# Two-operand VectorE steps of a routed two-layer network: `places` reckoned in a PSUM bank, `less` with an operand in PSUM, the sums of attention reduced

## The chip, the cores and the metric

The kernel runs on one core of one Trainium2 chip. The metric is the device time of one execution in microseconds (us). Names of engines in the profile: PE is TensorE's matmul, PEld its weight load, DVE is VectorE, ACT is ScalarE, POOL is GpSimd, SP is SyncE, which only issues DMAs here. SBUF is the large on-chip memory and PSUM the small one that TensorE writes to, in eight banks of 512 floats per partition.

## The reference, cut to what matters

`x` is (4, 384, 32, 32): four batches of 384 channels at 1024 places ("tokens"). There are two layers, each with a mixing part and a feed-forward part, all in float32:

```
x = x + scan(ln_channels(x))               # selective scan, 4 directions, 16 states, then a norm and gelu
t = tokens(x)
t = t + experts(ln_tokens(t))              # 4 experts, each token goes to its best 2
x = image(t)
x = x + attention(ln_channels(x))          # 8 heads of 64, queries = keys = values
t = tokens(x); t = t + kron_mlp(ln_tokens(t))
```

The routing, which the change touches most, is in the reference:

```
probs = softmax(scores)                    # over the 4 experts
topk_vals, topk_idx = top_k(probs, 2)
mask = sum(one_hot(topk_idx, 4))
masked = probs * mask
masked = masked / (sum(masked) + 1e-9)
out = einsum('bse,ebsd->bsd', masked, y)   # y: what each expert makes of the token
```

Attention is `softmax(w w^T / 8) w` for each head.

## The kernel before, in words

**Two streams.** `scan_layer` goes through 32 units (4 batches, 4 directions, 2 halves of 512 tokens). For each unit, `project` makes the step sizes, and `chunk` runs over three channel groups of 128 and four groups of four states. One step of `chunk` is: POOL multiplies `bx <- dtr, bcs` (L432), ACT makes `da` by an exponential into PSUM (L441), DVE scans along the tokens (L446), DVE (L453) or POOL (L460) multiplies by the output coefficients, and PE adds the states up in `acc` (L467). When a batch is through the scan, `finish` writes it to `x1`, and `tail_batch` of the batch before is handed in: `route` (transposes, norm, `places`, then scattered writes to `rows`), `experts` (11 slots of 256 or 128 tokens), `combine`, `prologue` (norm), `attention`, and `last_layers`. So the tail of batches 0 to 2 runs beside the scan of later batches, and the tail of batch 3, with what is left of batch 2's, runs alone at the end. `route` of batch b + 1 is handed in between `attention` and `last_layers` of batch b.

**Order.** The order of each engine's instructions is fixed before the run by a planner, which goes by the order of the program text, priorities (route, combine, prologue and last_layers have a raised one) and its own reckoning of durations. Each engine works its queue in order. A buffer or a bank of a pool is handed on when the planner has put its last reader behind it.

**Banks.** While the scan runs, it holds four of the eight PSUM banks. The tail has the other four: one double bank "s", one bank "o" and one bank "p" (`NARROW_BANKS`). Bank "o" is used by `y_ps` of the experts, `o_acc` of attention and `f_acc` of `last_layers` (L1165, copied out at L1170). Bank "p" is used by many short-lived tiles, among them `tt_ps` and `cnt_ps` of the route and every second `h_ps` of the experts. For batch 3, `route` takes its tiles and banks from a second set that opens when the scan's banks are free.

**What the change touches.**
- `less_mean` (L540 to L544) makes `-mean * rstd`, a 128x8 tile, in one DVE instruction, L543. It is called eight times: in `spread` of each route (L649, where ACT's L659 uses it) and in `prologue` of each batch (where ACT's L960 uses it, and the transposes L967 wait for that).
- `places` (L676 on) takes the scores `sc` (128 partitions x 8 blocks of tokens x 4 experts) and works out, in some 60 small DVE instructions, the softmax, each expert's rank for each token (L698 to L703 compare all pairs of experts), the two chosen ones, how many tokens before this one go to each expert (two matmuls, L718 and L719, and a running sum, L725), how many slots each expert fills (L729 to L743), and from that the row of every token in `rows` (`pos`, L788), its weight, and each slot's expert (L794 to L814). All of its tiles are in SBUF but the result of the two matmuls. L647 and L648, just ahead of it, finish the scores.
- `divide` in `attention` adds two sums of each token and head with one DVE instruction (L1028) and takes the reciprocal (L1029); four calls a batch.

Of the kernel before, what the change touches and what calls it, by code (L numbers as in the profile page):

```python
# [12 lines left out]
ALU = mybir.AluOpType  # L13
AX = mybir.AxisListType
# [3 lines left out]
P = 128  # L18
# [13 lines left out]
NE = 4  # L32
TOP = 2
# [15 lines left out]
MB = L // P  # L49
# [61 lines left out]
def halves(i):  # L111
    return slice(i * HF, (i + 1) * HF)


class Body:
# [424 lines left out]
    def less_mean(self, mean, rstd, room, tag):  # L540

        less = room.tile([P, MB], tag, "less")
        self.nc.vector.scalar_tensor_tensor(less, mean, -1.0, rstd, op0=ALU.mult, op1=ALU.mult)  # L543
        return less  # L544


# [129 lines left out]
    def places(self, sc, room):  # L676


        nc = self.nc
        nt = MB  # L680

        def over(v):
            return v.unsqueeze(2).to_broadcast([P, nt, NE])

        red = room.tile([P, nt], "g_red", "g_red")
        nc.vector.tensor_reduce(red, sc, AX.X, ALU.max)
        nc.vector.tensor_sub(sc, sc, over(red))
        nc.scalar.activation(sc, sc, AF.Exp)
        nc.vector.tensor_reduce(red, sc, AX.X, ALU.add)
        nc.vector.reciprocal(red, red)  # L690
        nc.vector.tensor_mul(sc, sc, over(red))

        shape = [P, nt, NE, NE]
        mine = sc.unsqueeze(3).to_broadcast(shape)
        other = sc.unsqueeze(2).to_broadcast(shape)
        above = room.tile(shape, "g_above", "g_above")
        same = room.tile(shape, "g_same", "g_same")
        nc.vector.tensor_tensor(above, other, mine, op=ALU.is_gt)  # L698
        nc.vector.tensor_tensor(same, other, mine, op=ALU.is_equal)
        nc.vector.tensor_mul(same, same, self.lower.unsqueeze(1).to_broadcast(shape))  # L700
        nc.vector.tensor_add(above, above, same)
        rank = room.tile([P, nt, NE], "g_rank", "g_rank")
        nc.vector.tensor_reduce(rank, above, AX.X, ALU.add)  # L703
        chosen = room.tile([P, TOP, nt, NE], "g_chosen", "g_chosen")
        for k in range(TOP):
            nc.vector.tensor_scalar(chosen[:, k], rank, float(k), None, op0=ALU.is_equal)
        nc.vector.tensor_scalar(rank, rank, float(TOP), None, op0=ALU.is_lt)
        nc.vector.tensor_mul(sc, sc, rank)
        nc.vector.tensor_reduce(red, sc, AX.X, ALU.add)
        nc.vector.tensor_scalar_add(red, red, 1e-9)  # L710
        nc.vector.reciprocal(red, red)
        nc.vector.tensor_mul(sc, sc, over(red))


        ps = room.bank("p", "cnt_ps")
# [1 line left out]
        flat = rank.rearrange("p m e -> p (m e)")  # L717
        nc.tensor.matmul(ps[:, :n], self.before, flat, start=True, stop=True)  # L718
        nc.tensor.matmul(ps[:, n : 2 * n], self.ones, flat, start=True, stop=True)  # L719
        cnt = room.tile([P, 2, nt, NE], "g_cnt", "g_cnt")  # L720
        nc.vector.tensor_copy(cnt.rearrange("p t m e -> p (t m e)"), ps[:, : 2 * n])
        run = room.tile([P, nt + 1, NE], "g_run", "g_run")
        nc.vector.memset(run[:, 0, :], 0.0)
        for m in range(nt):
            nc.vector.tensor_add(run[:, m + 1, :], run[:, m, :], cnt[:, 1, m, :])  # L725

        ns = nt * P // P
        need = room.tile([P, NE, ns], "g_need", "g_need")
        nc.vector.tensor_tensor(  # L729
            need, run[:, nt, :].unsqueeze(2).to_broadcast([P, NE, ns]),  # L730
            self.full[:, :ns].unsqueeze(1).to_broadcast([P, NE, ns]), op=ALU.is_gt,
        )

        used = room.tile([P, 2, NE], "g_used", "g_used")
        nc.vector.tensor_reduce(used[:, 1], need, AX.X, ALU.add)
        nc.vector.tensor_reduce(used[:, 0], need[:, :, 1::2], AX.X, ALU.add)
        nc.vector.scalar_tensor_tensor(
            used[:, 1], used[:, 0], -2.0, used[:, 1], op0=ALU.mult, op1=ALU.add
        )
        first = room.tile([P, 2, NE + 1], "g_first", "g_first")  # L740
        nc.vector.memset(first[:, :, :1], 0.0)
        for e in range(NE):
# [5 lines left out]

        at = cnt[:, 0]
        nc.vector.tensor_add(at, at, run[:, :nt, :])  # L750
        shift = room.tile([P, 2, NE], "g_shift", "g_shift")
        full, back = shift[:, 0], shift[:, 1]
        nc.vector.tensor_scalar(
            back, odd[:, :NE], float(NHALF) - 0.5, -float((NHALF + 2) * P), op0=ALU.is_gt, op1=ALU.mult
        )
# [5 lines left out]
            op0=ALU.mult, op1=ALU.add,  # L761
# [6 lines left out]
        ends = room.tile([P, nt, NE], "g_ends", "g_ends")  # L768
# [5 lines left out]
            at, pairs[:, :NE].unsqueeze(1).to_broadcast([P, nt, NE]), float(SLOT), at,  # L774
            op0=ALU.mult, op1=ALU.add,
        )
        nc.vector.tensor_add(at, at, ends)
        pick = room.tile([P, 2, TOP, nt, NE], "g_pick", "g_pick")
        both = [P, TOP, nt, NE]
        nc.vector.tensor_mul(pick[:, 0], chosen, at.unsqueeze(1).to_broadcast(both))  # L780
        nc.vector.tensor_mul(pick[:, 1], chosen, sc.unsqueeze(1).to_broadcast(both))
        picked = room.tile([P, 2, TOP, nt], "g_picked", "g_picked")
        nc.vector.tensor_reduce(
            picked.rearrange("p t k m -> p (t k m)"),
            pick.rearrange("p t k m e -> p (t k m) e"), AX.X, ALU.add,
# [1 line left out]
        pos = room.sb.tile([P, TOP, nt], I32, tag="g_pos", name="g_pos", bufs=2)  # L787
# [24 lines left out]
        )  # L812
        expert = room.sb.tile([P, NSLOT], I32, tag="g_expert", name="g_expert", bufs=2)
        nc.vector.tensor_copy(expert, ef)  # L814
        return pos, picked[:, 1], expert

    def experts(self, b, routed, room):

# [155 lines left out]
    def attention(self, xc, sums, room):  # L974
# [5 lines left out]
        nc, a = self.nc, self.a  # L980
# [44 lines left out]

        def divide(t, att):
            inv = room.tile([P, 2 * MB], "inv", "inv")
            nc.vector.tensor_add(inv, sums[:, t, :, 0], sums[:, t, :, 1])  # L1028
            nc.vector.reciprocal(inv, inv)  # L1029
            ps = room.bank("p", "inv_ps")  # L1030
            nc.tensor.matmul(ps[: 2 * MB, :P], inv, self.ident, start=True, stop=True)
            rows = room.tile([2 * MB, P], "inv_rows", "inv_rows")
            nc.vector.tensor_copy(rows, ps[: 2 * MB, :P])
            for i in range(NH):
                ps = room.bank("p", "bc_ps")
                for j in range(HF // P):
                    m = i * (HF // P) + j
                    for o in range(2):
                        at = 2 * m + o
                        nc.tensor.matmul(  # L1040
                            ps[o * HD : (o + 1) * HD, j * P : (j + 1) * P],
                            self.ident[: 2 * MB, at : at + 1].to_broadcast([2 * MB, HD]),
                            rows, start=True, stop=True,
                        )
                nc.vector.tensor_mul(att[:, halves(i)], att[:, halves(i)], ps)
# [370 lines left out]
```

## Time and profile before

| | |
|---|---|
| three runs | median 4451.01 us, 4446.85 to 4462.27 |
| the profiled execution | 4452.07 us, its span from first to last instruction 4450.2 |
| mean granted clock of TensorE | 0.850 |
| PE busy | 3462.1 us, 78% of the span |
| POOL busy | 3050.0 us, 69% |
| DVE busy | 2980.1 us, 67% |
| ACT busy | 2469.7 us, 55% |

| stretch of the trace | from, to (us) |
|---|---|
| last scan instruction of batch 3 (L446) | ends at 3564.6 |
| experts of batches 0, 1, 2, 3 (L889) | start at 935.1, 1995.2, 3046.3, 3696.4 |
| attention's scores of batches 0, 1, 2, 3 (L1015) | 1462 to 1767, 2520 to 2816, 3567 to 3931, 4195 to 4352 |
| `places` (L687 to L788) | 848 to 895, 1872 to 1918, 2927 to 2972, 3645 to 3661 |
| L543 in the prologues | starts at 1426.0, 2485.5, 3536.3, 4176.5 |

A line of the profile such as "L453 DVE TENSOR_TENSOR bx<-da,bcs" names the line of the kernel, the engine, the operation, the tile that is written and the tiles that are read. Busy time does not tell of waiting inside an instruction: an instruction that has begun and can't go on counts as busy, and only its length gives it away.

### The profile page before, as it was taken

To read this page: it belongs to the slowest core of one execution; us is meant where nothing else is said; L and a number is where in the kernel's file an instruction comes from. 1 tells how busy PE (TensorE), PEld (TensorE's weight loads), DVE (VectorE), ACT (ScalarE), POOL (GpSimd) and SP (SyncE) were. 2 spreads that over 40 slices of the span, in tenths; PEclk is the share of its full clock that TensorE was granted. 3 is DMA by queue.
4 is the path that set the end of the run, shared out by engine and by line. 5 is a ranking of instruction groups with operands and counts; after the bars stand their busy time and mean duration, and the time that the engine had idled before them with its cause. 6 is when DMAs were issued, how large, how long until landed. Compare 5 with 4: busy or idle time off the path is not lost. (4 is left out here: it accounts for less than half of the span.)

```text
span 4450.2 us, 47090 instructions
## 1 busy us (share of the span) xinstructions
PE 3462.1 (78%) x13980; PEld 1644.5 (37%) x13980; DVE 2980.1 (67%) x4252; ACT 2469.7 (55%) x4380; POOL 3050.0 (69%) x1475
## 2 busy tenths in 40 slices
PE   6545554579995887669998688758998699999897
PEld 2111111245552222325555222214555334566333
DVE  5889998778887876978787777988787720020002
ACT  4545554456664766466666477466666453325354
POOL 4999999689988877779888689879888710000100
PEclk7766665579997998679999899869999899999898
DMA  4444453468785533357779434446778534344300
GB/s 121 119 124 114 129 162 91 134 225 233 217 253 169 164 93 116 117 174 217 209 229 274 134 99 120 123 145 193 215 212 261 171 106 139 123 135 164 102 17 15
DMA packets 404760, 684.81 MB, mean 154 GB/s; under 512 B 50960, under 2 KB 206480, under 8 KB 404496
## 3 DMA queue, kind: packets, MB, share of 16 engines
q1 hardware_dynamic: 395184, 655.37, 50.0%
q0 software_dynamic: 8192, 25.17, 1.7%
q8 instruction: 112, 1.84, 0.2%
q14 instruction: 152, 1.25, 0.1%
q10 hardware_dynamic: 1120, 1.18, 0.1%
HBM read 561.47 MB, written 120.06 MB: 153 GB/s over the span
## 5 line engine op out<-in xcount | busy, mean ns | idle before, releaser
L432 POOL TENSOR_TENSOR bx<-dtr,bcs 128x1024 f32<-128x1024 f32 x768 | 1793.5, 2362 | 211.5 <-PE acc L467 118.2
L441 ACT ACTIVATE da<-dtr,nega 128x512 f32<-128x512 f32 x1536 | 1045.8, 691 | 1013.9 <-DVE bx L453 637.7
L460 POOL TENSOR_TENSOR bx<-bx,bcs 128x1024 f32<-128x1024 f32 x384 | 904.0, 2360 | 216.9 <-DVE bx L446 94.9
L467 PE MATMUL acc<-bx,sel 128*32 128x512 f32 x3072 | 518.6, 712 | 304.2 <-POOL bx L460 258.4
L889 PE MATMUL h_ps<-xc,w 128*128 128x256 f32 (+1 forms) x3168 | 665.2, 364 | 43.6 <-DVE xc L871 21.1
L905 PE MATMUL y_ps<-w,hs 128*128 128x384 f32 x1824 | 644.1, 505 | 44.3 <-ACT hs L898 40.3
L889 PEld LDWEIGHTS h_ps<-xc,w 128*128 128x128 f32 x3168 | 547.4, 196 | 228.6 <-issue 92.0
L446 DVE TENSOR_TENSOR_SCAN bx<-da,carry,bx 128x512 f32<-128x512 f32 x384 | 473.9, 1269 | 125.1 <-ACT da L441 61.9
L446 DVE TENSOR_TENSOR_SCAN da<-da,carry,bx 128x512 f32<-128x512 f32 x384 | 477.3, 1273 | 70.6 <-ACT da L441 61.3
L446 DVE TENSOR_TENSOR_SCAN bx<-da,bx 128x512 f32<-128x512 f32 x384 | 451.8, 1209 | 102.6 <-POOL bx L432 61.3
L453 DVE TENSOR_TENSOR bx<-da,bcs 128x512 f32<-128x512 f32 x768 | 511.3, 680 | 4.5
L446 DVE TENSOR_TENSOR_SCAN da<-da,bx 128x512 f32<-128x512 f32 x384 | 455.7, 1219 | 74.5 <-ACT da L441 62.9
L905 PEld LDWEIGHTS y_ps<-w,hs 128*128 128x128 f32 x1824 | 348.6, 196 | 339.6 <-issue 78.2
L1020 ACT ACTIVATE ex<-s_ps 128x512 f32<-128x512 f32 x512 | 299.2, 590 | 207.1 <-PE s_ps L1015 206.1
L1015 PE MATMUL s_ps<-w 64*128 64x512 f32 x1024 | 307.6, 675 | 83.0 <-ACT ex L1020 83.0
L467 PEld LDWEIGHTS acc<-bx,sel 128*32 128x32 f32 x3072 | 78.6, 116 | 606.1 <-POOL bx L460 371.0
L1064 PE MATMUL o_acc<-ex,vt 128*64 128x512 f32 x1024 | 295.3, 657 | 0.6 <-ACT att L1072 0.5
L894 ACT ACTIVATE hs<-h_ps,bb 128x256 f32<-128x256 f32 (+1 forms) x528 | 193.6, 449 | 148.5 <-PE h_ps L889 148.3
L1105 POOL TENSOR_TENSOR xt<-xt,wb 128x3072 f32<-128x3072 f32 x4 | 26.7, 6686 | 310.4 <-DMA wb<-in_wb 310.4
L909 DVE TENSOR_TENSOR y<-y_ps,bb 128x384 f32<-128x384 f32 x76 | 41.6, 548 | 244.0 <-PE y_ps L905 244.0
L926 POOL TENSOR_TENSOR diag<-ident,g_picked 128x1024 f32<-128x1024 f32 x8 | 15.0, 1895 | 243.1 <-PE xc_ps L868 223.8
L1015 PEld LDWEIGHTS s_ps<-w 64*128 64x128 f32 x1024 | 80.9, 192 | 257.6 <-ACT ex L1020 153.4
(215 smaller groups left out, 4026.3 us busy)
## 6 DMA issues: line engine op xcount, KB each, us to landing
w<-in_w SPq DMA_DIRECT2D x352, 576.0 KB
dtr<-dd SPq DMA_DIRECT2D x1536, 128.0 KB
bcs<-rows SPq DMA_DIRECT2D x512, 128.0 KB
dd<-one_e SPq DMA_DIRECT2D x96, 256.0 KB
dd<-mag SPq DMA_DIRECT2D x96, 256.0 KB
rows<-zero SPq DMA_DIRECT2D x76, 192.0 KB
xs<-rows SPq DMA_DIRECT2D x32, 384.0 KB
made<-y SPq DMA_DIRECT2D x32, 384.0 KB
```

The costliest lines, as they stand in the source:

```text
L432: pool = nc.gpsimd.tensor_mul(bx, dtr[q][1], bc[:, 0].unsqueeze(1).to_broadcast([P, 2, HF])).ins
L441: nc.scalar.activation(da, dtr[q][0][:, j, :], AF.Exp, scale=nega[:, col : col + 1])
L446: nc.vector.tensor_tensor_scan(run(h), run(da), run(bx[:, j, :]), 0.0 if first else hold, ALU.mult, ALU.add,)
L453: dve = nc.vector.tensor_mul(bx[:, j, :], h, cg).ins
L460: pool = nc.gpsimd.tensor_mul(bx, bx, cg.unsqueeze(1).to_broadcast([P, 2, HF])).ins
L467: nc.tensor.matmul(acc[lo : lo + DB, :], sel, out[q][:, j, :], start=(g == 0), stop=(g == NG - 1),)
L889: nc.tensor.matmul(ps[:, r, :], w1[(f + r) // wf][:, c, (f + r) % wf * P : ((f + r) % wf + 1) * P], xc[:, c, :], start=(c == 0), stop=(c = ...
L894: nc.scalar.activation(hs[:, f + r, :], ps[:, r, :], AF.Identity, bias=bb[:, f + r : f + r + 1])
L905: nc.tensor.matmul(out[:, :D], hs[:, f, t * P : (t + 1) * P], w2[f // wf][:, f % wf, :], start=(f == 0), stop=(f == FC - 1),)
L1015: nc.tensor.matmul(ps[:, o, :], w[rows, j * P : (j + 1) * P], w[rows, halves(i)], start=True, stop=True,)
L1020: ins = nc.scalar.activation(ex[:, o, :], ps[:, o, :], AF.Exp, scale=HD**-0.5, accum_out=sums[:, t, 2 * j + o, i : i + 1],).ins
L1064: ins = nc.tensor.matmul(out[cols, :], made[t][1][:, j, cols], ex[:, o, :], start=(j == 0), stop=(j == MB - 1),).ins
```

## The change

The change keeps what is computed. It alters where some small tiles lie and which instructions make them.

- `less_mean`: ScalarE first copies `rstd` into a tile of bank "p", and L543 reads it from there.
- `places`: a tile of bank "o" (`area`) is taken at the start, and `small` hands out pieces of it one behind the other. `red`, a second copy of the probabilities (`prob`, by one more multiplication), `same`, `number` (the rank before it becomes the mask), `chosen`, `cnt`, `total` (the last step of the running sum, which was the last row of `run`), `used`, `back` and `picked` lie there. What pairs with them stays or moves into SBUF: `sc`, `above`, `rank`, `part`, `run`, `need`, `blocks`, `first`, `full`, `row`, `ends`, `pick`. The weights that are returned are copied out to SBUF (`weight`), one more instruction.
- `divide`: the addition of two slices of `sums` becomes a reduction over its last axis, which has two elements.

```diff
     def less_mean(self, mean, rstd, room, tag):
         less = room.tile([P, MB], tag, "less")
-        self.nc.vector.scalar_tensor_tensor(less, mean, -1.0, rstd, op0=ALU.mult, op1=ALU.mult)
+        ps = room.bank("p", "less_ps")[:, :MB]
+        self.nc.scalar.copy(ps, rstd)
+        self.nc.vector.scalar_tensor_tensor(less, mean, -1.0, ps, op0=ALU.mult, op1=ALU.mult)
...
+        area = room.bank("o", "places")
+        used_up = [0]
+
+        def small(shape):
+            lo = used_up[0]
+            used_up[0] = lo + int(np.prod(shape[1:]))
...
-        red = room.tile([P, nt], "g_red", "g_red")
+        red, prob = small([P, nt]), small([P, nt, NE])
...
+        nc.vector.tensor_mul(prob, sc, over(red))
         nc.vector.tensor_mul(sc, sc, over(red))
...
-        other = sc.unsqueeze(2).to_broadcast(shape)
+        other = prob.unsqueeze(2).to_broadcast(shape)
         above = room.tile(shape, "g_above", "g_above")
-        same = room.tile(shape, "g_same", "g_same")
+        same = small(shape)
...
-        nc.vector.tensor_reduce(rank, above, AX.X, ALU.add)
-        chosen = room.tile([P, TOP, nt, NE], "g_chosen", "g_chosen")
+        number = small([P, nt, NE])
+        nc.vector.tensor_reduce(number, above, AX.X, ALU.add)
+        chosen = small([P, TOP, nt, NE])
...
-        cnt = room.tile([P, 2, nt, NE], "g_cnt", "g_cnt")
+        cnt = small([P, 2, nt, NE])
...
-        for m in range(nt):
+        for m in range(nt - 1):
             nc.vector.tensor_add(run[:, m + 1, :], run[:, m, :], cnt[:, 1, m, :])
+        total = small([P, NE])
+        nc.vector.tensor_add(total, run[:, nt - 1, :], cnt[:, 1, nt - 1, :])
...
-        used = room.tile([P, 2, NE], "g_used", "g_used")
-        nc.vector.tensor_reduce(used[:, 1], need, AX.X, ALU.add)
+        used = small([P, 2, NE])
+        blocks = room.tile([P, NE], "g_blocks", "g_blocks")
+        nc.vector.tensor_reduce(blocks, need, AX.X, ALU.add)
...
-        shift = room.tile([P, 2, NE], "g_shift", "g_shift")
-        full, back = shift[:, 0], shift[:, 1]
+        full, back = room.tile([P, NE], "g_full", "g_full"), small([P, NE])
...
-        nc.vector.tensor_add(at, at, ends)
+        row = room.tile([P, nt, NE], "g_row", "g_row")
+        nc.vector.tensor_add(row, at, ends)
...
-        picked = room.tile([P, 2, TOP, nt], "g_picked", "g_picked")
+        picked = small([P, 2, TOP, nt])
...
-        return pos, picked[:, 1], expert
+        weight = room.tile([P, TOP, nt], "g_weight", "g_weight")
+        nc.vector.tensor_copy(weight, picked[:, 1])
+        return pos, weight, expert
...
         def divide(t, att):
             inv = room.tile([P, 2 * MB], "inv", "inv")
-            nc.vector.tensor_add(inv, sums[:, t, :, 0], sums[:, t, :, 1])
+            nc.vector.tensor_reduce(inv, sums[:, t], AX.X, ALU.add)
```

## The prediction

> **What bounds the kernel now.** I read the page's slices first, then the waits, then VectorE's (DVE's) rows one line at a time, and last the timeline of DVE and GpSimd (POOL) side by side.
>
> ```profile
> PE   6545554579995887669998688758998699999897
> ...
> DVE  5889998778887876978787777988787720020002
> ...
> POOL 4999999689988877779888689879888710000100
> ...
> ACT da L441 <- DVE bx L453: 637.7, 366, 9.8
> ```
>
> The first three are tenths of busy time in 40 slices of 111 us. Up to slice 32 (about 3600 us) the scan runs, DVE and POOL mostly at 7 to 9 tenths, neither full for long; after that TensorE is full and DVE and POOL stand nearly still. The last row, the longest wait, says who paces the scan: ScalarE idles 637.7 us until DVE frees a `da` buffer. So a microsecond that DVE loses before 3600 us is mostly lost to the end, and one after it hardly counts.
>
> DVE does lose some. The rows are min/median/max of one instruction in ns:
>
> ```profile
> L453 DVE TENSOR_TENSOR bx<-da,bcs x768: 649/679/696, 57.3 to 3564.6; 128x512 f32<-128x512 f32 x192
> ...
> L543 DVE SCALAR_TENSOR_TENSOR less<-mv,rstd x8: 152/164/12677, 847.6 to 4176.5; 128x8 f32<-128x8 f32 x8
> ...
> L1028 DVE TENSOR_TENSOR inv<-sums x16: 174/176/10531, 1535.6 to 4353.1; 128x16 f32<-128x16 f32 x16
> ...
> L743 DVE TENSOR_TENSOR g_first<-g_first,g_used x16: 145/163/2278, 879.8 to 3658.3; 128x2 f32<-128x2 f32 x16
> ```
>
> L453 reads `da` in PSUM and `bcs` in SBUF, 768 times beside a busy POOL, and never leaves 649 to 696 ns. The others have both operands in SBUF, and on eight, sixteen or two elements one takes up to 12.7 us. The timeline round the longest (start, length, then idle time before in brackets), DVE above, POOL below:
>
> ```profile
> 1426.00 12.68 DVE L543 SCALAR_TENSOR_TENSOR less<-mv,rstd 128x8 f32<-128x8 f32 x1 [0.61 <-ACT rstd L151]
> 1438.60 2.44 DVE L446 TENSOR_TENSOR_SCAN bx<-da,carry,bx 128x512 f32<-128x512 f32 x2
> ...
> 1425.90 4.63 POOL L432 TENSOR_TENSOR bx<-dtr,bcs 128x1024 f32<-128x1024 f32 x2
> 1430.51 1.25 POOL L388 TENSOR_TENSOR lnw<-lnw,mag 128x512 f32<-128x512 f32 x1
> 1431.73 6.92 POOL L432 TENSOR_TENSOR bx<-dtr,bcs 128x1024 f32<-128x1024 f32 x3
> 1441.19 2.35 POOL L460 TENSOR_TENSOR bx<-bx,bcs 128x1024 f32<-128x1024 f32 x1 [2.54 <-DVE bx L446]
> 1452.02 2.37 POOL L460 TENSOR_TENSOR bx<-bx,bcs 128x1024 f32<-128x1024 f32 x1 [8.48 <-DVE bx L446]
> ```
>
> DVE's 8-element instruction stands while POOL runs six in a row and ends as that run ends; then POOL starves for 2.54 and 8.48 us, waiting for the scans that DVE could not start. [...]
>
> **The change, part by part.** A stall below is a row's length less the shortest of its kind, from DVE's timeline. Only rows before 3600 us stall.
>
> *`less` (L543).* The four of the routes take 0.15 us; three of the prologues take 12.68, 11.62 and 10.80, stalls of 12.5, 11.5 and 10.6. With `rstd` in PSUM they have one SBUF operand, as L453. POOL worked meanwhile, so I count only what it idles afterwards: 11.0 (2.54 + 8.48), 8.8 (3.35 + 5.44) and 12.2, capped at 10.6: **30.4 us**. ScalarE's L960 of the layer behind the scan ("the tail") waits for `less` too (12.79 us idle), so both streams gain.
>
> *`inv` (L1028).* A reduce reads one operand. Its stalls are 1.7, 1.2, 2.2, 0.3 and 10.4 us; POOL idles 8.50 behind the last; of the other 5.4 I take half, the ends being 0 and 5.4: **11.2 us**. The reduce costs as the add (nearest row: L689's reduce, 166 ns, against 176).
>
> *`places`.* Each call has some 37 DVE instructions with two SBUF operands; five stay so (the two of L794, L806, L809, L810), and L647 ahead of it. Stalls that go: 15.0 us in the first call (L687, L698, L708, L743, L763 and others), 12.6 in the second, 15.3 in the third, none in the fourth, where POOL is idle. The three stretches, and one of the experts:
>
> ```profile
> core 0: us, PE busy (x) PEld busy (x) DVE busy (x) ACT busy (x) POOL busy (x), PEclk, DMA share, GB/s
> 843.00:897.00 54.00, 16.84 (x38) 3.54 (x38) 53.43 (x110) 21.12 (x35) 37.41 (x19) 0.56 0.31 91
> 1859.00:1920.00 61.00, 24.63 (x76) 7.00 (x78) 58.67 (x100) 29.83 (x43) 35.63 (x18) 0.53 0.27 74
> 2917.00:2974.00 57.00, 23.96 (x78) 6.76 (x78) 56.38 (x115) 29.42 (x43) 37.04 (x18) 0.62 0.20 58
> 1000.00:1400.00 400.00, 353.07 (x1528) 205.91 (x1526) 330.17 (x443) 263.29 (x420) 360.83 (x168) 0.95 0.78 228
> ```
>
> DVE is full in all three (53.43 of 54), so a stall there is time. POOL is late next: it reaches 360.83/400 = 0.90 where it is busiest, so the stretches can't shrink below 37.41/0.9 = 41.6, 39.6 and 41.2 us, which caps the gains at 12.4, 21.4 and 15.8: 12.4 + 12.6 + 15.3 = **40.3 us**.
>
> Gains: 30.4 + 11.2 + 40.3 = 81.9 us.
>
> *Costs.* (1) PSUM access: about 50 instructions of a call now touch PSUM. Low end: a copy of one element out of PSUM (L452) and one out of SBUF (L457) both have a median of 148 ns, so 0. High end: L909, 384 elements with one operand in PSUM, 548 ns, against L1098, 384 in SBUF, 496 at shortest: 0.052 us. The latter are two-operand forms as most of `places` is; 50 x 0.052 = 2.6 a call, 10.4 in four. The fourth lies on the chain that ended last. [...] (2) Two more instructions a call (`prob`, the copy of `weight`), 0.19 each: 1.2 in three calls. (3) `places` lies in one tile, so what ran in step may follow one by one: rows between 3658.3 and 3660 start 0.06 to 0.10 apart, a dependent chain (L725) 0.20; some 20 such rows, 0 to 2 us in the fourth call, say 1. (4) ScalarE's copy before `less`: 0.2 as L151 (0.21), and a handover, 0.3 on the path of four prologues: 1.5 with the routes; its bank "p" was last used 60 us before (the expert's last h_ps ends at 1362.8), so no wait. (5) The five forms left: the 42.9 us are 28 stalls in three calls, so 9 in 37 instructions and 1.5 us each (a few are one-operand copies and scalings from SBUF to SBUF, L706, L707, L710, L788; L759 stays such a one and no gain is claimed for it); 5 x 9/37 x 1.5 = 1.9 a call, 6 in three. Ends 0 and 22 (every one, 5 x 1.5 x 3). (6) `places` now holds the only bank "o" of the scan phase. The first `f_acc` matmul (L1165) starts at 1908.1 and about 2955.5, the calls end at 1917.9 and 2971.8: it would wait 9.8 and 16.3 us. With the stalls gone the calls end near 1905 and 2956.5, so about 0 and 1. Ends 0 and 26; I take 6, since the planner issues behind `f_acc` the copies on DVE (L1170) and then the outputs, and the next experts' gather stands behind those outputs on SyncE's queue (xs at 1987.2). POOL's queue is not passed by anything.
>
> Sum of costs: 10.4 + 1.2 + 1 + 1.5 + 6 + 6 = 26. Net 82 - 26 = 56 us. The profiled execution took 4452.07 (span 4450.2), the median is 4451.01; 4452 - 56 = 4396, and 1 less from the median: **4395 us**.
>
> **Rivals.** *POOL takes the place of DVE.* After a freed `less`, DVE catches up with POOL's lead and waits for bx, POOL being at 0.9 in the experts; or the stalls move to L647 and the five forms left. For it: neither engine is full over the scan, and DVE waited 121.2 us for POOL's bx already. Against: POOL is 0.62 busy in the three stretches. Half the gains, the same costs: 41 - 26 = 15, about 4436. If all of the gains were taken back by waiting it is a change that doesn't do what it says, 4451.
>
> *Slower: bank "o".* The planner, which fixes every engine's order beforehand, gives the bank to `places` first and puts `f_acc` and all behind it after the whole call; or an `o_acc` of attention ends up behind it. Price: the tail late by one stretch, 54 to 61 us, twice, 115, against 82 - 20 = 62 gained: about +53, 4504. It decides once the waits for the bank pass 62 us in all. For it: one bank, three users, DVE's in-order `fy` already idles 59.8 us for `f_acc`. Against: attention ends at 1775 and 2821, before `places` starts.
>
> **Chances.** The forecast, 4360 to 4425: at one end all 93 us of the stalls (34.6 + 15.8 + 42.9) come back for costs (2) and (4), at the other the bank costs its 26 and half the forms stall, 82 - 26 - 20 - 5 = 31 left, some 4421: 0.58. POOL's half, 4425 to 4438: 0.12. Within 0.3% (13 us, about what a measurement of this kernel can tell from no change), from costs that meet the gains: 0.12. Slower: 0.18. So faster 0.70, same 0.12, slower 0.18; the range reaches from 4355, just past the forecast's best end, to 4470, just into the slower case, so that about 2 in 10 lie outside.
>
> **What would show it.** Right: L543's and L1028's longest row near their median; in `places` only L647, L794 to L810 and L759 above 1 us; the three stretches near 42 to 48 us with DVE still full; the last scan row at about 3510 instead of 3564.6. Wrong: long waits for `f_acc` on PE, `fy` on DVE, or POOL's idle time up by what DVE gained. The forecast fails if the scan ends earlier but the attention left over behind it, on a full TensorE, grows by as much.

## The result, and the profile after

| | before | after |
|---|---|---|
| median of 20 runs each, on one chip | 4452.26 us | 4463.70 us |
| after / before | | 1.0022 [1.0013, 1.0031] |
| span of the profiled execution | 4450.2 us | 4459.1 us |
| DVE busy | 2980.1 us | 2905.9 us |
| POOL busy | 3050.0 us | 3050.9 us |

So the kernel became about 11 us slower, where 56 us less were forecast. The slices of after (PE, DVE, POOL, 40 slices of 111 us) look like those of before:

```profile
PE   6545554479997787669998788758898789999997
...
DVE  5889998768886785978787577888778620002102
...
POOL 5999998788989787779898579878888720000100
```

The rows of the changed lines in after (min/median/max of one instruction in ns) show that the stalls went:

```profile
L453 DVE TENSOR_TENSOR bx<-da,bcs x768: 640/680/695, 57.0 to 3532.2; 128x512 f32<-128x512 f32 x192
...
L545 DVE SCALAR_TENSOR_TENSOR less<-mv,less_ps x8: 149/158/164, 846.3 to 4185.8; 128x8 f32<-128x8 f32 x8
...
L1051 DVE TENSOR_REDUCE inv<-sums x16: 163/186/189, 1505.8 to 4362.3; 128x16 f32<-128x32 f32 x16
...
L764 DVE TENSOR_TENSOR g_first<-g_first,places x16: 147/158/160, 871.7 to 3645.8; 128x2 f32<-128x2 f32 x16
```

The longest `less` is 164 ns instead of 12677, the longest `inv` 189 instead of 10531. The timeline of after round the first prologue's `less` (start, length, in brackets idle time before, and what ended it), DVE above, POOL below:

```profile
1404.94 0.16 DVE L545 SCALAR_TENSOR_TENSOR less<-mv,less_ps 128x8 f32<-128x8 f32 x1 [0.24 <-ACT less_ps L544]
1405.02 2.45 DVE L446 TENSOR_TENSOR_SCAN bx<-da,carry,bx 128x512 f32<-128x512 f32 x2
1411.91 2.47 DVE L446 TENSOR_TENSOR_SCAN da<-da,carry,bx 128x512 f32<-128x512 f32 x2 [4.44 <-ACT da L441]
...
1400.81 6.98 POOL L432 TENSOR_TENSOR bx<-dtr,bcs 128x1024 f32<-128x1024 f32 x3
1407.74 1.27 POOL L388 TENSOR_TENSOR lnw<-lnw,mag 128x512 f32<-128x512 f32 x1
1408.97 4.65 POOL L432 TENSOR_TENSOR bx<-dtr,bcs 128x1024 f32<-128x1024 f32 x2
```

`less` passes in 0.16 us in the middle of an unbroken run of POOL. But the next scans are soon done, and DVE then idles 4.44 us: it has run into the next wait.

That is what the waits say of the whole scan. A line gives who waited for what: us in total, times, longest. Before:

```profile
ACT da L441 <- DVE bx L446: 285.6, 359, 5.8
...
DVE bx L446 <- POOL bx L432: 121.2, 60, 9.9
```

After:

```profile
ACT da L441 <- DVE bx L453: 615.6, 380, 10.7
...
ACT da L441 <- DVE bx L446: 310.3, 384, 17.6
...
DVE bx L446 <- POOL bx L432: 185.9, 86, 15.3
...
DVE fy L1193 <- PE f_acc L1188: 78.5, 7, 24.9
```

DVE's busy time fell by 74.2 us, and its wait for POOL's `bx` rose by 64.7. ScalarE's longest wait for DVE (L453) fell by 22.1, but its second one (L446) rose by 24.7: with 637.7 + 285.6 = 923.3 us before and 925.9 after, ScalarE waits for DVE as long as it did. DVE's wait for `f_acc` rose from 59.8 to 78.5; 17.8 us of it lie in batch 1, where there was none before. The milestones (us; `places` is taken from L648, which finishes the scores, to the end of `pos`, and `z_ps` from the start of its last row):

| | before | after | difference |
|---|---|---|---|
| last scan instruction on DVE ends | 3564.6 | 3531.7 | -33 |
| last product of the scan on POOL (L460) ends | 3563.9 | 3552.1 | -12 |
| experts of batch 3 start | 3696.4 | 3684.7 | -12 |
| `places` of batches 0, 1, 2 takes | 47.5, 46.7, 48.0 | 38.0, 51.8, 49.9 | -9.5, +5.1, +1.9 |
| `z_ps` to first `f_acc`, batches 0, 1 | 36.7, 31.8 | 53.2, 53.8 | +17, +22 |
| experts of batches 1, 2 take | 446.8, 450.6 | 451.9, 456.2 | +5, +6 |
| experts of batch 2 start | 3046.3 | 3056.0 | +10 |
| attention's scores of batch 2 start | 3566.8 | 3582.2 | +15 |
| from the start to the end of batch 3's experts | 449.3 | 469.8 | +20.5 |
| of that, PE idle | 3.3 | 15.4 | +12 |
| span | 4450.2 | 4459.1 | +9 |

The scan's end gained 12 us, the tail of the earlier batches came 10 to 15 us later, and behind the scan, where TensorE should be full, 20.5 us were lost: 12 of them as idle gaps of PE. Nearly all of the rest is work of batch 2 that was still to do. The tail is not late by the bank alone: the experts of batches 1 and 2 also took 5 to 6 us longer each. In bank_p they are back at 446.1 and 450.1, but in places_p, which has no hold either, they take 454.9 and 457.3, so the cause of that part is open. Two windows of 380 us behind the scan (us and instruction counts of PE, PEld, DVE, ACT, POOL, then the granted clock, the share of full speed that TensorE was given), before:

```profile
3720.00:4100.00 380.00, 379.59 (x1581) 230.87 (x1580) 40.84 (x76) 154.90 (x277) 6.67 (x1) 1.00 0.41 132
```

and after, with the three stretches of `places` ahead of it:

```profile
843.00:887.00 44.00, 13.58 (x38) 3.19 (x38) 43.15 (x116) 20.84 (x35) 38.58 (x19) 0.60 0.46 123
1859.00:1920.00 61.00, 30.18 (x84) 7.46 (x84) 59.55 (x112) 36.78 (x53) 39.33 (x20) 0.53 0.32 103
2917.00:2977.00 60.00, 25.45 (x76) 6.71 (x80) 58.94 (x130) 35.03 (x51) 38.33 (x19) 0.50 0.31 98
...
3720.00:4100.00 380.00, 367.91 (x1510) 218.58 (x1509) 41.41 (x79) 130.60 (x280) 6.68 (x1) 1.00 0.39 122
```

The clock is 1.00 in both to two digits (after has one stretch of 3.41 us at half clock, worth 1.7 us), so PE's 379.59 against 367.91 is idle time, not a slower PE. In the stretches of batches 1 and 2 DVE is as full as before, with 112 and 130 instructions instead of 100 and 115 (the last window is 60 us long, before's was 57): what `places` saved was filled with scans (22 and 20 of them inside it instead of 14 and 15), since the planner lays `places` and the scan into one queue by its own reckoning. DVE's own time in `places` fell from 26.9, 23.5 and 26.0 to 14.4, 15.9 and 18.2 us, yet `pos` was ready at 1917.0 and 2976.1, against 1917.9 and 2971.8.

The bank shows in TensorE's timeline. The first `f_acc` matmul before, batches 0 and 1:

```profile
1908.14 2.78 PE L1165 MATMUL f_acc<-hs,wc 128*32 128x512 f32 x10 [2.59 <-ACT hs L1157]
...
2955.50 3.41 PE L1165 MATMUL f_acc<-hs,wc 128*32 128x512 f32 x12 [1.30 <-ACT hs L1157]
```

and after:

```profile
1917.11 3.25 PE L1188 MATMUL f_acc<-hs,wc 128*32 128x512 f32 x12 [5.28 <-DVE g_weight L837]
...
2976.28 3.63 PE L1188 MATMUL f_acc<-hs,wc 128*32 128x512 f32 x12 [3.82 <-DVE g_weight L837]
```

Before, it waited for its operand `hs`; after, for `g_weight`, the last reader of `places`' bank "o". The bracket holds only PE's idle time; the start itself is 9 and 21 us later.

### The profile page after: what moved, and what is told of

It reads as the page before. It is cut to its first block, busy times and chain, and to the rows that moved or that the text cites. A ratio compares the mean times of both kernels' runs of the same rounds, so it can differ in the third digit from the quotient of the medians.

```text
span 4459.1 us, 47100 instructions
## 1 busy us (share of the span) xinstructions
PE 3484.7 (78%) x13980; PEld 1657.3 (37%) x13980; DVE 2905.9 (65%) x4260; ACT 2472.4 (55%) x4386; POOL 3050.9 (68%) x1475
## 3 DMA queue, kind: packets, MB, share of 16 engines
q14 instruction: 152, 1.25, 0.1%
## 4 chain that ended last, share of the span: by engine, by line
PE 28%; DVE 10%; ACT 6%; POOL 4%; issue 3%; DMA 3%; SPq 1%; DVEq 0%; POOLq 0%; ACTq 0%
PE y_ps L928 7%; PE h_ps L912 6%; PE s_ps L1038 4%; PE o_acc L1087 3%; DVE da L446 3%; DVE bx L446 3%; POOL bx L432 2%; PE w_ps L1015 1%; DVE bx L453 1%; PE acc L467 1%; ACT da L441 1%; ACT hs L921 1%; PE o_ps L1135 1%; DMA w<-in_w 1%; PE f_acc L1188 1%
## 5 line engine op out<-in xcount | busy, mean ns | idle before, releaser
L460 POOL TENSOR_TENSOR bx<-bx,bcs 128x1024 f32<-128x1024 f32 x384 | 903.3, 2357 | 198.3 <-DVE carry L457 93.9
L467 PE MATMUL acc<-bx,sel 128*32 128x512 f32 x3072 | 501.0, 705 | 281.3 <-POOL bx L460 244.9
L912 PE MATMUL h_ps<-xc,w 128*128 128x256 f32 (+1 forms) x3168 | 674.2, 367 | 49.1 <-DMA w<-in_w 18.3
L446 DVE TENSOR_TENSOR_SCAN bx<-da,carry,bx 128x512 f32<-128x512 f32 x384 | 473.7, 1270 | 143.7 <-POOL bx L432 91.9
L446 DVE TENSOR_TENSOR_SCAN bx<-da,bx 128x512 f32<-128x512 f32 x384 | 453.0, 1210 | 150.3 <-POOL bx L432 94.0
L446 DVE TENSOR_TENSOR_SCAN da<-da,carry,bx 128x512 f32<-128x512 f32 x384 | 477.3, 1273 | 66.7 <-ACT da L441 64.1
L453 DVE TENSOR_TENSOR bx<-da,bcs 128x512 f32<-128x512 f32 x768 | 510.5, 680 | 3.8
L446 DVE TENSOR_TENSOR_SCAN da<-da,bx 128x512 f32<-128x512 f32 x384 | 454.8, 1219 | 44.4 <-ACT da L441 31.3
L357 PE MATMUL dt_ps<-xd,wdt 12*128 12x512 f32 x192 | 125.6, 739 | 71.9 <-ACT mag L396 37.1
```

The source lines that it names most:

```text
L446: nc.vector.tensor_tensor_scan(run(h), run(da), run(bx[:, j, :]), 0.0 if first else hold, ALU.mult, ALU.add,)
L453: dve = nc.vector.tensor_mul(bx[:, j, :], h, cg).ins
L460: pool = nc.gpsimd.tensor_mul(bx, bx, cg.unsqueeze(1).to_broadcast([P, 2, HF])).ins
L467: nc.tensor.matmul(acc[lo : lo + DB, :], sel, out[q][:, j, :], start=(g == 0), stop=(g == NG - 1),)
L912: nc.tensor.matmul(ps[:, r, :], w1[(f + r) // wf][:, c, (f + r) % wf * P : ((f + r) % wf + 1) * P], xc[:, c, :], start=(c == 0), stop=(c = ...
```

## The experiments

Each group of four ran on one chip, with runs of the kernel before between them, and each ratio is to those (medians of before: 4475.07, 4453.65 and 4471.79 us). Diffs are against the kernel before unless it is said otherwise, and cut to the lines that matter.

**Is it the bank, or are the stalls worth nothing?** First the parts alone, the whole change with another bank, and the bank's hold alone.

*`less` and `inv` alone* (label less_inv), the diff's parts in `less_mean` and `divide`:

```diff
+        ps = room.bank("p", "less_ps")[:, :MB]
+        self.nc.scalar.copy(ps, rstd)
+        self.nc.vector.scalar_tensor_tensor(less, mean, -1.0, ps, op0=ALU.mult, op1=ALU.mult)
...
+            nc.vector.tensor_reduce(inv, sums[:, t], AX.X, ALU.add)
```

> Parts one and three of the change alone (less with rstd in PSUM, the sums reduced); places as before. Theory A (the end is set by the tail, and places in bank o holds f_acc and so hands back what less and inv gain): 4405 to 4430 us, since nothing holds the bank. Theory B (microseconds freed on DVE are worth nothing, because POOL and the fixed order pace both streams): 4445 to 4460, although the 34.6 us of stalls of less are gone from the rows.

Measured: 4482.53 us, ratio 1.0013 [1.0003, 1.0024]. DVE's busy time fell by 41 us (2938.9), and there was no gain at all: batch 3's experts took 475.1 us with PE idle 16.2 of them. So the bank is not the whole story; a loss behind the scan comes without it too, though how much `less` and `inv` would gain without that loss stays open.

*`places` alone* (places_only): the change with `less_mean` and `divide` as before.

```diff
+        area = room.bank("o", "places")
```

> Part two of the change alone (places in bank o); less and inv as before. Theory A: slower than the whole change, 4470 to 4490, since the bank costs and less does not pay. Theory B: between the kernel before and the whole change, 4450 to 4465.

Measured: 4506.66 us, 1.0072 [1.0055, 1.0089]. Alone, this part is clearly a loss. The parts do not add up: with `less` and `inv` added, the whole change loses less (1.0022).

*The whole change with the two banks exchanged* (bank_p), against the kernel after:

```diff
-        area = room.bank("o", "places")
+        area = room.bank("p", "places")
...
-        ps = room.bank("p", "cnt_ps")
+        ps = room.bank("o", "cnt_ps")
```

> The whole change, but places lies in bank p and the short-lived cnt_ps in bank o, so that f_acc has to wait only for cnt_ps. Theory A: f_acc no longer waits for the copy of weight, it starts within 45 us of z_ps in batches 0 and 1 (53 and 54 in the whole change, 37 and 32 before), and the time falls to 4415 to 4440. Theory B: f_acc starts earlier and the time stays at 4455 to 4465.

Measured: 4474.04 us, 1.0002 [0.9993, 1.0011]. `f_acc` follows z_ps by 30.6 and 30.8 us again, so the bank's wait is gone; but PE idles 18.6 us in batch 3's experts, and the time is that of before.

*The hold alone* (hold_o): the kernel before, with `places` in SBUF, and a tile of bank "o" that is written after the first maximum and read at the end. It adds two small instructions to a call.

```diff
+        hold = room.bank("o", "hold")[:, :nt]
+        nc.vector.tensor_scalar(hold, red, 0.0, None, op0=ALU.mult)
...
-        return pos, picked[:, 1], expert
+        weight = room.tile([P, TOP, nt], "g_weight", "g_weight")
+        nc.vector.tensor_add(weight, picked[:, 1], hold.unsqueeze(1).to_broadcast([P, TOP, nt]))
+        return pos, weight, expert
```

> The kernel before, with places as it was in SBUF, but a tile of bank o is written behind the first maximum and read again when the weights are picked (two more small DVE instructions, the same computation), so that the bank is held as in the change and no operand is moved. Theory A: 4465 to 4500, the price of the bank without the gains. Theory B: 4450 to 4458.

Measured: 4503.48 us, 1.0064 [1.0050, 1.0078], which is 0.0064 x 4475 = 28 us. TensorE's timeline names the wait:

```profile
1917.71 2.77 PE L1169 MATMUL f_acc<-hs,wc 128*32 128x512 f32 x10 [14.92 <-DVE g_weight L818]
```

PE idles 14.92 us there and 17.76 before the same matmul of batch 1. But most of the 28 us is again lost in batch 3's experts, which take 474.2 us instead of 449.3: PE idles 16.8 us in them (3.3 in before), and the granted clock falls to half five times for 3.41 us, which costs another 8.5 us and does not happen in before's. So this run shows the wait, but it does not give the price of the bank.

**What is a microsecond of each stream worth?** The second group made one stream late on purpose, and asked how well one profile repeats.

*The kernel before once more* (before_again), nothing changed.

> The kernel before, unchanged, so that its trace lies on the same chip as the others of this group: no difference. Both theories: ratio 1.000 within 0.002.

Measured: 4455.82 us, 1.0005 [0.9992, 1.0018]. Its profiled span was 4440.1 us, 10.1 shorter than the first profile's, and from the experts of batch 1 on every milestone is 10 to 11 us earlier: from there the lengths between milestones repeat to a few tenths, the absolute times don't. The 12 us that the scan's end gained, and the 10 to 15 us that the tail lost, are therefore hardly more than two profiles of one kernel differ by; only ratios of many runs, and lengths, carry a verdict.

*The tail late* (tail_late): the first projection of attention of batch 2 waits for the scan's last gelu.

```diff
+                    ins = nc.tensor.matmul(
...
+                    if self.late is not None:
+                        self.depend(ins, self.late)
```

> The kernel before, with one dependency more: the first projection of attention in batch 2 waits for the last gelu of the scan, so that this attention starts some 35 to 45 us later (its scores at about 3605 instead of 3567) while the scan is free to end as it did. Theory C (after the scan TensorE is full, so the end is what is left over of the tail: a tail late by d costs 0.75 d, a scan late by d only 0.25 d, as the whole change shows: scan end and last experts 12 us earlier, attention of batch 2 15 us later, last experts done 9 us later): 26 to 34 us slower, ratio 1.006 to 1.008. Rival S (the scan's end and the route of batch 3 set the end): within 8 us of before, 0.998 to 1.002, or faster.

Measured: 4486.46 us, 1.0076 [1.0053, 1.0099]. Against before_again's profile the attention scores of batch 2 start 43 us later, the experts of batch 3 start 2 us later and end 39 us later. Nearly all of the 43 us seems to arrive at the end, and the ratio lies in the range of theory C. But of the 36.5 us by which these experts take longer, 14.8 are more idle time of PE and 3.4 are lost at half clock, so lateness alone explains about half of what was measured.

*The scan late* (scan_late): the scattered writes of the last route wait for the second quarter of batch 2's attention.

```diff
+                if b == B - 1:
+                    self.depend(put, self.second)
```

> The kernel before, with one dependency more: the scattered writes of the last route wait for the reciprocal of the second quarter of attention in batch 2, which is done at about 3697, 35 us after the writes begin now. So the last experts begin about 35 us later and the tail of batch 2 is not held. Theory C: 0.25 x 35 = 9 us slower, ratio 1.002 (1.000 to 1.004). Rival S: 35 us slower, 1.008.

Measured: 4472.70 us, 1.0041 [1.0026, 1.0055]. The experts of batch 3 start 29.9 us later and end 29.9 us later: the weights expected here, a quarter for the scan and three quarters for the tail, did not hold. The experts took as long as before, 449.3 us, though less of attention was left for them (1841 instructions of PE instead of 1947), because PE idled 18.4 us instead of 3.3 and the clock was halved five times for 3.41 us, 8.5 us more. Each of the five begins within 4.1 us of the start of a gap of more than 1 us; not every gap has one. A hundred us of the stretch, first in before_again, then in scan_late (us; busy time and instructions of PE, PEld, DVE, ACT, POOL; then the granted clock):

```profile
3800.00:3900.00 100.00, 100.00 (x411) 56.73 (x410) 6.79 (x12) 38.98 (x88) 6.68 (x1) 1.00 0.41 134
```

```profile
3800.00:3900.00 100.00, 95.74 (x356) 54.19 (x352) 5.27 (x8) 35.93 (x79) 6.67 (x1) 0.97 0.39 127
```

Idle time and clock together are 23.6 us, about what the expectation let the experts save (three quarters of 29.9, 22.4). So its weights are neither shown nor refuted. The waits of PE say what the gaps are:

```profile
PE y_ps L907 <- ACT hs L900: 14.8, 7, 4.0
```

*`places` alone with the banks exchanged* (places_p):

```diff
+        area = room.bank("p", "places")
...
+        ps = room.bank("o", "cnt_ps")
```

> places in bank p with cnt_ps in bank o, and less and inv as before: the moved operands of places alone, without the hold of bank o. If the moved operands are worth what the stalls in the three stretches say (40 us): 0.991 to 0.994. If the planner hands the time to the scan and the tail gets none (theory C): 0.998 to 1.004, with places as long as before in batches 1 and 2 (45 to 52 us) and more scan instructions in it (18 to 22 instead of 14 and 15).

Measured: 4471.21 us, 1.0041 [1.0025, 1.0057]. Without the hold `places` alone loses less than with it (1.0072; the two intervals just touch), but still loses. Against before_again's profile the attention of batch 2 starts 9 us earlier, the last product of the scan ends 22 us later, and PE idles 15.5 us in batch 3's experts. In this order the tail got ahead at the expense of the scan.

**The gaps behind the scan.** Of the eight kernels so far with another order, seven have the same 11.5 to 14.8 us of PE waiting for `hs` (places_only has 4.7). Two such lines, in the stretch 3680 to 4160 us, before:

```profile
PE y_ps L905 <- ACT hs L898: 2.7, 2, 2.2
```

after:

```profile
PE y_ps L928 <- ACT hs L921: 14.8, 8, 2.1
```

and ScalarE at the first of them in after:

```profile
3708.64 1.28 ACT L921 ACT_TABLE_LOAD   x1
3709.93 2.77 ACT L921 ACTIVATE hs<-hs 128x3072 f32<-128x3072 f32 x1
```

The gelu of a slot is one instruction of 2.77 us behind a table load of 1.28, and the slot's first `y_ps` waits for all of it, 2.13 us. Where the planner puts another matmul there (most slots in before) nothing is lost; where its new order does not (after), 2.13 us are lost for a slot. The third group gives the last batch's gelu in two halves, so that `y_ps` can begin after the first.

*The kernel before with halves* (before_half):

```diff
-            self.exp_again(nc.scalar.activation(hs, hs, AF.Gelu).ins)
+            if b < B - 1:
+                ins = nc.scalar.activation(hs, hs, AF.Gelu).ins
+            else:
+                for f in range(0, FC, FC // 2):
+                    part = hs[:, f : f + FC // 2, :]
+                    ins = nc.scalar.activation(part, part, AF.Gelu).ins
+            self.exp_again(ins)
```

> The kernel before, with the gelu of each slot of the last batch's experts in two halves, so that the first y_ps can start on the first half; all that runs before the last experts is planned as it was. Theory D (behind the scan the plan of the kernel before happens to leave TensorE idle for only 3.3 of the 449 us of the last experts, while every plan that was drawn up anew leaves 15 to 19, mostly 2.13 us before a slot's first y_ps, waiting for gelu): hardly anything to win here, ratio 0.998 to 1.002. Rival (the gap is filled by chance elsewhere and the halves help every plan alike): 0.996 to 0.998.

Measured: 4473.06 us, 0.9996 [0.9986, 1.0006]. Nothing to win where there are no gaps. Its profile (span 4472.0) can stand for the kernel before on this chip.

*The whole change with halves* (after_half): the same edit to the kernel after.

```diff
+                for f in range(0, FC, FC // 2):
```

> The whole change with the same edit. Theory D: the 14.8 us that PE waits for hs in the last experts fall to 5 or less, 8 to 11 us of the change's loss come back, ratio 0.999 to 1.001 instead of 1.0022. Rival: the gaps are not what the end waits for (the attention left over is): 1.002 to 1.004 although the gaps close.

Measured: 4478.16 us, 1.0016 [1.0007, 1.0026]. PE's idle time there fell from 15.4 to 0.9 us, and the experts took 456.2 us instead of 469.8, but the time hardly moved (1.0022 to 1.0016): what was left of batch 2 now comes behind the experts, 60 us from their end to the scores of batch 3 instead of 50. From the start of these experts to the end of the span it is 774.3 us as it was 774.4.

*Banks exchanged and halves* (bank_p_half), against the kernel after: both edits.

```diff
-        area = room.bank("o", "places")
+        area = room.bank("p", "places")
...
+                for f in range(0, FC, FC // 2):
```

> The whole change with places in bank p and cnt_ps in bank o, and the same edit. Theory D with the bank theory: 0.997 to 0.999, the first of these kernels to be faster than before. If neither bank nor gaps hold the end: 1.000 to 1.002 as without the halves.

Measured: 4446.59 us, 0.9944 [0.9930, 0.9957]. So with both losses away the change is a gain of 25 us. These three profiles are of one chip; the kernels differ in the change and the bank alone, and in what the planner makes of that:

| | before_half | after_half (bank "o") | bank_p_half |
|---|---|---|---|
| span | 4472.0 | 4478.4 | 4440.8 |
| POOL's idle time up to the scan's last product | 577.4 | 570.1 | 552.2 |
| that product ends | 3572.3 | 3567.5 | 3548.8 |
| experts of batch 1 start | 2000.3 | 2012.2 | 2003.4 |
| experts of batch 1 end | 2444.4 | 2467.1 | 2448.3 |
| experts of batch 2 start | 3054.9 | 3071.3 | 3038.9 |
| scores of batch 2 start | 3575.2 | 3597.6 | 3554.0 |
| experts of batch 3 start | 3715.9 | 3704.1 | 3685.1 |
| experts of batch 3 take (PE idle) | 448.9 (3.1) | 456.2 (0.9) | 450.8 (1.3) |

DVE's waits, before_half:

```profile
DVE bx L446 <- POOL bx L432: 112.5, 61, 9.9
```

and bank_p_half:

```profile
DVE bx L446 <- POOL bx L432: 182.2, 79, 15.3
```

Even here DVE's busy time fell by 69 us (2979.2 in before_half, 2909.9) and its wait for POOL rose by 70. POOL's idle time fell by 25.2; as POOL's busy time up to there is the same within 3 us, that is the earlier end of the scan said once more, and single profiles of one kernel differ by 10 us in it. The last column against the middle one is the exchange of the banks with all that follows from it: 32 us at the start of batch 2's experts and 4478.16 - 4446.59 = 31.6 us at the end. Not all of it is waiting for the bank. The experts of batch 1 start 9 us later and take 10 us longer, and the last `z_ps` of batch 1, ahead of the second hold, is already 26 us late. The mean granted clock differs too: 0.844 over the runs of after_half, 0.847 over those of bank_p_half, 0.848 over those of the kernel before. In the three groups' runs of the kernel before, which all have one order, a clock lower by 0.001 went with 1 to 2.3 us more, so as an estimate the clock may hold 4 to 8 of the 31.6 us; whether it is a cause or follows from the order is open. One way from the bank to the next experts can be read in SyncE's queue. After_half:

```profile
3057.33 0.37 SPq L1214 DMA_DIRECT2D out<-out  x1
3060.80 0.36 SPq L1214 DMA_DIRECT2D out<-out  x1
3063.97 0.38 SPq L882 DMA_DIRECT2D xs<-rows  x1
```

Bank_p_half:

```profile
3028.04 0.36 SPq L1214 DMA_DIRECT2D out<-out  x1
3030.91 0.38 SPq L882 DMA_DIRECT2D xs<-rows  x1
3032.05 0.34 SPq L1214 DMA_DIRECT2D out<-out  x1
```

The outputs of batch 1 (behind `fy`, behind `f_acc`, which follows `z_ps` 23 us later than in bank_p_half) stand ahead of the gather `xs` for the experts of batch 2. The scattered writes to `rows`, which the gather reads, are issued some 50 us earlier in both kernels, so it is the queue that the gather stands in. But rows of the scan stand in that queue as well, so that it is the outputs that hold it up is likely and not shown.

*Banks exchanged, halves, and the product of `z` in one instruction* (bank_p_half_z), against bank_p_half:

```diff
-        for r in range(nq):
-            nc.vector.tensor_mul(
-                z4[:, :, r, :], zt, rstd.unsqueeze(2).to_broadcast([P, MB, KR])
-            )
+        four = [P, MB, nq, KR]
+        nc.vector.tensor_mul(
+            z4, zt.unsqueeze(2).to_broadcast(four),
+            rstd.unsqueeze(2).unsqueeze(3).to_broadcast(four),
+        )
```

> The same, and in the last layers z4 is made by one DVE instruction instead of four with two SBUF operands each (the same computation), which stalled by 2.15 us each in batches 0 and 1, on the tail's own chain. If a stall on the tail's chain is worth its length there: some 6 us a batch in batches 0 and 1, so 0.994 to 0.997. If the planner hands it to the scan again: 0.997 to 1.000.

Measured: 4439.37 us, 0.9933 [0.9919, 0.9946], the fastest of all. The four instructions (L1154 in after) had stalled up to 2.15 us each in `last_layers` of batches 0 and 1. One large instruction stalls once (1225 to 2621 ns, four calls). The scan's last product ends 20 us earlier (3528.4), but from the start of the last experts to the end it is 773.2 us instead of 755.7, so most of that is lost again. The interval overlaps with that of bank_p_half, so the step between the two is likely but not shown.

## Why the prediction was wrong

**The stalls went, as forecast.** Rows of `less`, `inv`, `g_first`: right. The sum of DVE's stalls (rows more than 0.5 us above the shortest of their kind) fell from 119 to 47 us. Some came up elsewhere, on instructions that the change does not touch: `z` from 9.0 to 14.4 us in all, `wc` (L1098, now L1121) from 1.9 to 6.5, and in bank_p_half one `wc` takes 12.7 us.

**They were not worth their time: the first step that failed.** It reads "So a microsecond that DVE loses before 3600 us is mostly lost to the end". The gains were set at 30.4 + 11.2 + 40.3 = 81.9 us, from the time that POOL idled behind each stall. Less the costs (1) to (5), 20 us, the forecast without a bank was 62. With the bank exchanged and the gaps closed the change gains 25 us. This is the mechanism of the rival "POOL takes the place of DVE", which the prediction gave half the gains: freed, DVE waits for POOL's `bx` 65 to 70 us longer. The line "ACT da <- DVE bx" was read as the pace of the scan, but it names only the last in a chain of three engines that wait for each other, each idle a part of the time, and ScalarE's waits for DVE did not shrink: 923.3 us before, 925.9 after, 942.0 in bank_p_half. The row for DVE waiting for POOL, 121.2 us, stands in the prediction, but only as a point for that rival. Its point against it, POOL 0.62 busy in the three stretches, is 0.64 by the rows shown there. POOL's idle time behind one stall was also no clean price: without the stall the next wait stands in its place, as the 4.44 us in the timeline above.

**`places`: the time went to the scan.** "The three stretches near 42 to 48 us": 38.0, 51.8 and 49.9. DVE's own time in them fell by 28 us, where stalls of 42.9 were to go. But in batches 1 and 2 the planner laid more scans between the small instructions, so the bank was held no shorter than the old calls had lasted. The cap of 0.9 of POOL's time, by which this was reckoned, took the order as given.

**Cost (6), the bank "o", was the cost most wrong.** It was 6 us, with ends of 0 and 26. `f_acc` itself came 16.5 and 22 us later behind `z_ps` where about 0 and 1 were forecast, and exchanging the banks is worth 31.6 us between after_half and bank_p_half, 9 between after and bank_p (1.0022 and 1.0002); the part of it that is waiting can't be split off. The path starts as described, at `f_acc` and `fy`; its further part, the outputs and the gather, is likely. The size failed because the forecast let the call end at 1905 and 2956.5 "with the stalls gone", and it ended at 1917.0 and 2976.1. The rival "Slower: bank 'o'" named this mechanism and put its point at 62 us of waits, that is, gains less costs; with 25 us of net gain the point lies at some 25, and the exchange of 31.6 us passes it.

**The unforeseen step: a new order behind the scan.** The sum took all that lies behind 3600 us as unchanged. The planner draws the order behind an edit anew, and the order before happens to leave PE 3.3 us idle in batch 3's experts; after and the seven other kernels of the first two groups that changed the order had 7.6 to 18.6. The clock adds to it: half clock cost 0 us there in before, 1.7 in after and up to 10.2 (less_inv). Four kernels hold the whole change:

| ratio to before | bank "o" | bank "p" |
|---|---|---|
| gelu whole | 1.0022 | 1.0002 |
| gelu in halves | 1.0016 | 0.9944 |

The kernel before with halves is at 0.9996. Bank_p to bank_p_half shows that the gaps alone can make a verdict: these experts took 473.4 us and then 450.8, of which 17.3 are idle time and 5.1 half clock. The two edits are not additive: after to after_half gained only 0.0006, as what was left of batch 2 came behind the experts. So how many us of the 11 belong to the bank and how many to the gaps stays open; the sum does not split. That 4463.70 us lies within the stated 4355 to 4470 is no support for the working: about 11 us were lost, where 56 were to be gained.

**The other costs.** (1) PSUM access was 10.4 us and hardly shows in the rows: `less` has a median of 158 ns with one operand in PSUM and 164 before, and the fourth call, which has no stalls, takes 11.6 us of DVE against 11.2, some 0.4 for about 50 instructions and the two more of cost (2), where 2.6 were set. (5) The forms left with two SBUF operands, and the casts beside them, stalled by 5.2, 4.7 and 7.1 us in the three calls, 17 instead of 6, within its ends of 0 and 22. No run here tells (2) to (4) from nothing.

**What would show it.** "The last scan row at about 3510" was 3531.7, and even that says too much, since the last product of the scan on POOL ended at 3552.1. The sign given for failure, long waits for `f_acc` on PE and `fy` on DVE, was there (`fy` 59.8 to 78.5 us), but the total of `fy` alone is no proof of the bank: scan_late, which has no hold, shows 78.9, there behind the scan. The last sentence's sign was there in part: the scan ends earlier, and the attention left over grows, but as much again went into gaps.

## What to carry to other kernels

A stall that goes is worth what the next engine in the chain stops idling, so before crediting it read who waits for whom in the whole ring, here ScalarE for DVE and DVE for POOL, and don't credit all of it: here 25 of 62 us, net of costs, came through. Under a planner that fixes the order, ask what it will do with the freed time, and compare the order behind the edit as well: an edit to one stage moved gaps of 2 us into a stage 700 us later. Look at the granted clock there too, since some gaps were followed by half clock (five times 3.41 us in scan_late). A scarce bank that is taken for a long, in-order stretch holds its next user up (PE idled 14.92 us before `f_acc` in hold_o), and likely what is queued behind that; exchange it with one whose users are short before giving up the idea.

## What the runs showed of the hardware

- A DVE instruction with two operands in SBUF waited through a whole run of POOL instructions, 12.68 us over six of them (`less` of batch 0 in before; five of some 2.3 us and one of 1.25), not only through the one under way; with one of the two operands in PSUM none of the 768 of L453 (640 to 696 ns in before and after) nor the eight of `less` (149 to 164 ns in after) did.
- Two forms with a single SBUF operand that write to SBUF were not free of it: `g_full` (L779, a scaling of four elements) took up to 2058 ns against 138 at shortest in after, the cast `g_pos` (L788) up to 2060 against 158 in before. Both of these longest ones ended within 0.1 us of the end of a POOL instruction (at 2960.7 and 2971.7 us).
- An operand in PSUM cost a small DVE instruction nothing that can be measured here (a median of 158 ns in after against 164 in before for `less`).
- Gaps of TensorE in a stretch that otherwise kept it full were in part followed by 3.41 us at half the granted clock: five such stretches in the 449.3 us of scan_late's last experts, one in the 469.8 us of after's, none in before's. In the one of after most `y_ps` matmuls took 847 ns instead of 486.
- Two profiles of one unchanged kernel differed by 10 us at every milestone from batch 1's experts on, while the lengths between them agreed to a few tenths.
